# Block 1 of a two-layer kernel: a unit's first outputs move into the next step, v is transposed one key step later, and TensorE's order is tied to the step list

## The chip, the cores and the metric

The kernel runs on one core of a Trainium2 chip. A core has TensorE (matmuls, shown as PE in the profile, with its weight loads as PEld), VectorE (DVE), ScalarE (ACT), GpSimd (POOL), and SyncE (SP), whose queue issues the DMAs here. The engines run independently, each through its own instructions in a fixed order, and wait for one another by semaphores. SBUF is the working memory; TensorE writes its results to PSUM, which has eight banks. The metric is device time of one execution in microseconds, less is better.

## What is computed

Two layers over x of 4 sequences of 256 tokens, 512 wide: a gated linear attention with decay, a router with a bias mix, a state-space mixer and an adapter layer. The change is in the first, "block 1":

```python
q = (hidden_states @ Wq.T).reshape(B, L, H, D)          # H = 32 heads, D = 128
k = (hidden_states @ Wk.T).reshape(B, L, KVH, D)        # KVH = 8
v = (hidden_states @ Wv.T).reshape(B, L, KVH, D)
q, k = _apply_rope(q, cos, sin), _apply_rope(k, cos, sin)
dt = jax.nn.softplus(hidden_states @ Win.T + dt_bias)
g = dt * -jnp.exp(A_log_bias)
G = cumsum of g within chunks of 128
scores = einsum('bhnid,bhnjd->bhnij', q, k)
decay = where(causal, exp(G_i - G_j), 0)
y_intra = einsum('bhnij,bhnjd->bhnid', scores * decay, v * dt)
y = y_intra + (what earlier chunks carry over, with its decay)
y = y / sqrt(mean(y * y) + eps) * gnorm_w
gate = (hidden_states @ Wg.T).reshape(B, L, H, D)
y = y * silu(gate)
return y.reshape(B, L, H * D) @ Wo.T                    # added to x
```

With two chunks in a sequence, the carry-over of the second chunk is written as one more block of scores with its own decay.

## The kernel before

**Arithmetic.** Matrices are split into a high and a low part in a reduced fp32 format, and a product is three matmuls (high·high, high·low, low·high). `split` (line 128) makes the parts of a weight: a cast on ScalarE (line 135), a subtraction on GpSimd (line 138). `Weights` (line 142) is a list in order of use; a call such as `u.w.o()` splits everything up to that weight and starts the loads of the next two (lines 169 to 178). The step W does nothing in block 1, since `due` stays at −1 there.

**Units and steps.** Block 1 is `retention` (line 299). The tokens are in two halves of 512. A unit is a key/value group g, a pair of heads hp of its four, and a half: 32 units. For g below 5 the halves alternate; for the last three groups all units of half 0 come first, then all of half 1 (lines 460 to 468). The loop at line 495 goes over steps i from −1 to 32, with `before`, `u` and `after` the units i−1, i and i+1, and walks through a list of step names, `STEP1`, or `SIDE1` while there is side work (`k.side`):

- S0, S1, S2 (`scores`, line 387): a block of scores of u in six matmuls, into PSUM tag y; VectorE multiplies them into the decays `m` (line 400).
- A0, A1 (`value`): `attend` multiplies by v into tag g (line 408); `square` takes ScalarE's squares, GpSimd's power and VectorE's product `yr` (lines 421 to 426).
- N0, N1 (`norm`): four transposes into tag y (line 433), VectorE's product with the gate `r` (line 436), a cast on ScalarE and a subtraction (lines 439, 440).
- F (`finish(u, 0)`) and C (`finish(before, 1)`): 12 matmuls with Wo in two groups of tag o (line 452) and two VectorE additions to x (line 456). F is in u's own step, C in the next one.
- K: one step of `keys` (line 356) for `after`, where it needs a new k and v: first the k projection and its rotation, then the v projection, its copy to SBUF (line 363) and four transposes (line 366) with a copy (line 368).
- Q0, Q1 (`queries`): projection of `after`'s queries (12 matmuls at line 197, tag x), rotation by three VectorE operations and a GpSimd addition (`rope`, lines 341 to 354), and a cast and a subtraction into the one tile `qs`.
- G0, G1 (`gate`): projection of `after`'s gates, copied by ScalarE (line 383); U is their silu; D (`ready`, `decays`) loads cumulated decays to all partitions (`gb`, line 283), adds and masks them into `m` and takes the exponential (line 376).
- P and T (`k.pump`): a step of side work: the router of a finished half and the preparation of the next block, put into `k.side` by `close` when a half is done (from step 26 on).

**What sets the order.** The program is traced in the order above; a scheduler then places every instruction on its engine by a simulated timeline: among those whose inputs and buffers are free, the one that comes first in the program. So program order is a priority, and the order that an engine gets can be another one. Tiles of a pool and tag share a number of buffers; each PSUM tag (x, y, g, o) has two banks. ScalarE's functions through `k.act` (line 1111) are tied to program order in groups: silu needs one function table, exp and ln another, a table load (line 1115) stands at each change, and `behind` (line 1106) keeps each group behind the load and the load behind the group before it. `order` (line 1099) is how such a tie is made: it binds the scheduler and adds no semaphore.

Of the kernel before, what the change touches and what calls it, by code (L numbers as in the profile page):

```python
# [18 lines left out]
P = 128  # L19
# [10 lines left out]
AHEAD = 0  # L30
BANK1, BANK3 = "o", "x"
LATE = (0, 3)
STEP1 = "S0 S1 S2 W C K P A0 A1 K Q0 T P W Q1 W K P N0 G0 P W N1 G1 U T W F T D".split()
SIDE1 = "S0 T S1 P S2 W C P K A0 T A1 K Q0 P W T Q1 W P K N0 G0 P T N1 G1 U W T P F T D W".split()
STEP3 = "W T0 T1 B I0 W M0 M1 X0 X1 I1 O0 G0 W W O1 W W P O2 W W G1 P W O3 D0 D1 W W".split()
FILL3 = "B X0 X1 I0 I1 P P G0 G1 W W P P W D0 D1 E E".split()
SIDE3 = "T0 T1 I0 I1 M0 M1 P B X0 X1 P P O0 W O1 G0 G1 W W P O2 O3 W P W P D0 D1 E E".split()
# [147 lines left out]
def chunk(w, n):  # L185

    return [part[:, n, :].rearrange("p (c m) -> p c m", c=KC) for part in w]


def proj(k, tc, w, half, name, tag="x"):  # L190

    ps = k.psum.tile([P, FREE], F32, tag=tag, name=f"ps_{name}")
    x = k.xs[half]
    terms = [(w[0], x[0]), (w[0], x[1]), (w[1], x[0])]
    for c in range(KC):
        for n, (a, b) in enumerate(terms):
            tc.nc.tensor.matmul(  # L197
                ps, a[:, c, :], b[:, c, :], start=(c == 0 and n == 0), stop=(c == KC - 1 and n == 2)
            )
    return ps  # L200


# [96 lines left out]
def retention(k, tc, io, arrive, begun, done, tail):  # L299
# [3 lines left out]
    nc = tc.nc  # L303
    NH, NG = 32, 8
    with ExitStack() as st:
# [5 lines left out]
        n = 2 * NH * 2  # L311
        at = 2 * SEQ
# [43 lines left out]
        def keys(g, half, w):  # L356

            nm = f"{g}_{half}"
            kk = [k.wk.tile([P, FREE], F32R, tag="a", name=f"k{part}_{nm}", bufs=4) for part in "hl"]
            rope(proj(k, tc, chunk(w, 0), half, f"k_{nm}"), *kk, f"k_{nm}")  # L360
            yield
            vT = k.wk.tile([P, FREE], F32, tag="sq", name=f"vT_{nm}", bufs=1)
            nc.scalar.copy(vT, proj(k, tc, chunk(w, 1), half, f"v_{nm}"))
            ps = k.psum.tile([P, HT, P], F32, tag="x", name=f"ps_vt_{nm}")
            for t in range(HT):
                nc.tensor.transpose(ps[:, t, :], vT[:, t * P:t * P + P], k.ident)
            v = k.wk.tile([P, HT, P], F32, tag="sg", name=f"v_{nm}", bufs=4)
            nc.scalar.copy(v, ps)
            kv[half] = kk, v
            yield  # L370
# [7 lines left out]
        def queries(u, w, h):  # L378
            nm = f"q_{u.name}_{h}"
            rope(proj(k, tc, chunk(w, h), u.half, nm), qs[:, 0, h, :], qs[:, 1, h, :], nm)  # L380
# [6 lines left out]
        def scores(u, blk):  # L387

            kh, kl = u.kk
            zj, zi = ((0, 0), (1, 1), (0, 1))[blk]  # L390
            ps = k.psum.tile([P, 4, P], F32, tag="y", name=f"ps_sc_{u.name}_{blk}")
            for b in range(2):
                aj = slice((2 * b + zj) * P, (2 * b + zj) * P + P)
                ai = slice((2 * b + zi) * P, (2 * b + zi) * P + P)
                for i, (a, q) in enumerate(((kh, 0), (kh, 1), (kl, 0))):
                    nc.tensor.matmul(  # L396
                        ps[:, b::2, :], a[:, aj], qs[:, q, :, ai], start=(i == 0), stop=(i == 2)
                    )
            m = u.m[:, blk]
            nc.vector.tensor_tensor(m, m, ps, ALU.mult)  # L400

        def attend(u, z):
            blocks = (((0, 0),), ((0, 2), (1, 1)))[z]
            nm = f"{u.name}_{z}"
            ps = k.psum.tile([P, 4, P], F32, tag="g", name=f"ps_y1_{nm}")
            for q in range(4):
                for i, (zj, blk) in enumerate(blocks):
                    nc.tensor.matmul(  # L408
                        ps[:, q, :], u.m[:, blk, q, :], u.v[:, 2 * (q % 2) + zj, :],
                        start=(i == 0), stop=(i == len(blocks) - 1),  # L410
                    )
            u.ps_y[z] = ps

        def square(u, z):
# [13 lines left out]
        def norm(u, z):  # L428

            nm = f"{u.name}_{z}"  # L430
            ps_t = k.psum.tile([P, 4, P], F32, tag="y", name=f"ps_yt1_{nm}")
            for q in range(4):
                nc.tensor.transpose(ps_t[:, q, :], u.yr[z][:, q, :], k.ident)
            r = k.wk.tile([P, 4, P], F32, tag="yh", name=f"r1_{nm}", bufs=YB)
            sg = u.sg.rearrange("p h (b z l) -> p z (h b) l", b=2, z=2)[:, z]
            nc.vector.scalar_tensor_tensor(r, ps_t, gnorm, sg, ALU.mult, ALU.mult)
            hi = k.wk.tile([P, 4, P], F32R, tag="y", name=f"yh1_{nm}", bufs=4)
            lo = k.wk.tile([P, 4, P], F32R, tag="y", name=f"yl1_{nm}", bufs=4)
            nc.scalar.copy(hi, r)
            nc.vector.tensor_tensor(lo, r, hi.bitcast(F32), ALU.subtract)  # L440
            u.y[z] = hi, lo

        def finish(u, z):
            wh, wl = u.w.o()
            yh, yl = u.y[z]
            for b in range(2):
                t = HT * u.half + 2 * b + z
                ps = k.psum.tile([P, HID], F32, tag="o", name=f"ps_o1_{u.name}_{z}{b}")
                i = 0
                for h in range(2):  # L450
                    for y, w in ((yh, wh), (yh, wl), (yl, wh)):
                        nc.tensor.matmul(  # L452
                            ps, y[:, 2 * h + b, :], w[:, h, :], start=(i == 0), stop=(i == 5)
                        )
                        i += 1
                nc.vector.tensor_add(k.x[t], k.x[t], ps)

# [2 lines left out]
        for gs in [[g] for g in range(NG - LONE1)] + [range(NG - LONE1, NG)]:  # L460
# [3 lines left out]
            for g, hp, half in unit:  # L464
                u = Ctx()
                u.g, u.hp, u.half, u.h0, u.name = g, hp, half, 4 * g + 2 * hp, f"{g}_{hp}_{half}"
                u.ps_y, u.yr, u.y = {}, {}, {}
                units.append(u)

        before, uses = None, []  # L470
        gnorm = k.small([P, 1], "gnorm")
        for n, u in enumerate(units):

            if before is not None and (before.g, before.hp) == (u.g, u.hp):
                u.w = before.w
            else:
                u.w = w = Ctx()
                at = u.g, u.hp
                if u.hp == 0:
                    uses.append((n - 1, 0, w, "kv", io["L0_kv"][u.g], u, "w"))  # L480
                uses.append((n - 1, 1, w, "q", io["L0_attn_Wq"][at], u, "w"))
                uses.append((n - 1, 2, w, "g", io["L0_attn_Wg"][at], u, "w"))
                uses.append((n, 3, w, "o", io["L0_attn_Wo"][at], u, "wo"))
            before = u

        for _, _, w, n, src, u, tag in sorted(uses, key=lambda one: one[:2]):
# [8 lines left out]
        for i in range(-1, len(units) + 1):  # L495
            before, u, after = (
                units[j] if 0 <= j < len(units) else None for j in (i - 1, i, i + 1)
            )
# [40 lines left out]
            def gate(u, h):  # L539
                if h == 0:  # L540
                    u.sg = only.tile([P, 2, FREE], F32, tag="sg", name=f"sg1_{u.name}")
                gates(u, u.w.g(), h, "x" if i >= 0 else "g")
# [4 lines left out]
            def value(z):  # L547
# [3 lines left out]
            k.bank = BANK1  # L551
            step = dict(
                S=lambda z: scores(u, z), G=lambda h: i < 0 or gate(after, h), U=silu, A=value,
                N=lambda z: norm(u, z), F=lambda: finish(u, 0), C=close,
                Q=lambda h: queries(after, after.w.q(), h),
                K=lambda: next(new, None), D=ready, P=k.pump, T=lambda: k.pump(1, True),
                W=k.weights.step,
            )
            if i < 0:
                gate(after, 0)  # L560
                gate(after, 1)
            for one in SIDE1 if k.side else STEP1:
                if tail and u is units[-1] and one in ("Q0", "G1", "Q1", "F"):
                    tail(("Q0", "G1", "Q1", "F").index(one))
                if tail and before is units[-1] and one in ("S1", "C"):
                    tail(("S1", "C").index(one) + 4)
                if u is None and one in ("P", "T") and i > 0:
                    continue
                who = {"C": before, "Q": after, "G": after, "U": after, "K": after, "D": after, "P": k, "T": k, "W": k}.get(one[0], u)
                if who is not None:  # L570
                    step[one[0]](*(int(z) for z in one[1:]))
            if i == 0:
                begun()

# [517 lines left out]
def tile_two_layers(ctx: ExitStack, tc: tile.TileContext, io: dict, out: bass.AP):  # L1092
    nc = tc.nc
    k = Ctx()
# [4 lines left out]
    def order(ins, before, reason):  # L1099
        tc.add_manual_dep(  # L1100
            ins.ins, before.ins.name,
            mybir.DependencyInfo(mybir.DependencyClass.NoSync, mybir.DependencyReason.DATA),
            reason=reason,
        )
# [30 lines left out]
            else:  # L1135
                steps -= 1

    k.act, k.small, k.pump, k.behind = act, small, pump, order
    k.n = 0
    k.const = ctx.enter_context(tc.tile_pool(name="const", bufs=1))  # L1140
    k.smalls = ctx.enter_context(tc.tile_pool(name="smalls", bufs=3))
    k.dram = ctx.enter_context(tc.tile_pool(name="dram", bufs=1, space=bass.MemoryType.DRAM))
# [14 lines left out]
    with tc.tile_pool(name="work", bufs=2) as k.wk:  # L1157

        k.room = k.wk.tile([P, 8 * SEQ], F32, tag="big", name="room")
        of = Ctx()  # L1160
# [92 lines left out]
```

## Time and profile before

| | |
|---|---|
| median of three runs | 2557.03 us (2550.06 to 2557.84) |
| the profiled execution | 2556.84 us, span 2555.1 us |
| mean granted TensorE clock | 0.987 |
| block 1 on TensorE | about 16 to 916 us |
| table loads of ScalarE | 193, 1.28 us each |
| DMA | 206 MB, 81 GB/s, engines busy 27% of the span |

The profile is one execution. Busy time is the time in which an engine was executing; matmuls overlap one another, so their mean duration (391 to 406 ns for 512 columns) is longer than the distance from one to the next (0.227 us at full clock). An idle time is put down to the instruction that ended it. The granted clock is the share of full speed at which TensorE was allowed to run. In block 1 matmuls of 512 columns are the bulk: queries, gates and outputs have 24 of them each in a unit.

### The profile page before, as it was taken

The numbers are of one execution on the slowest core, as the hardware profiler recorded it, in microseconds if no ns is written. First come the engines' busy times: TensorE is split into PE (matmuls) and PEld (weight loads), VectorE is DVE, ScalarE is ACT, GpSimd is POOL, SyncE is SP. The second block draws the span as 40 slices with busy tenths as digits, with TensorE's granted clock in tenths as the row PEclk, the third lists the DMA queues.
The fourth block names the chain that finished last, engine by engine and source line by source line (L and its number), as shares of the span: only waits on it lengthen the run. The fifth ranks groups of instructions, "written<-read, shape, count | busy, mean of one in ns | idle before, by whom it ended". The sixth has DMA issues, their size and how long they took to land.

```text
span 2555.1 us, 36947 instructions
## 1 busy us (share of the span) xinstructions
PE 2433.6 (95%) x14000; PEld 2009.3 (79%) x14000; DVE 2016.4 (79%) x2629; ACT 1475.9 (58%) x2365; POOL 1582.3 (62%) x1123
## 2 busy tenths in 40 slices
PE   7999999999989888899999999999999999999889
PEld 6888888887777776678878888888888888888677
DVE  7766666676668678688998988988988988989973
ACT  3645555555554545475765756656757656757631
POOL 4744645466566457576775774766856865857850
PEclk9999999999999998899999999999999999999999
DMA  3311212122231222232332232323223323223321
GB/s 107 106 53 42 67 50 66 50 73 85 83 89 48 70 84 86 76 120 74 99 97 69 84 90 80 95 67 99 87 79 92 90 67 91 92 71 110 92 79 68
DMA packets 82898, 206.26 MB, mean 81 GB/s; under 512 B 8673, under 2 KB 10593, under 8 KB 82721
## 3 DMA queue, kind: packets, MB, share of 16 engines
q1 hardware_dynamic: 82720, 203.90, 26.6%
q8 instruction: 111, 1.82, 0.3%
q14 instruction: 67, 0.54, 0.1%
HBM read 200.86 MB, written 3.01 MB: 80 GB/s over the span
## 4 chain that ended last, share of the span: by engine, by line
PE 61%; DVE 18%; POOL 9%; ACT 6%; issue 5%; DMA 1%; SPq 0%; POOLq 0%; ACTq 0%; DVEq 0%
PE ps_g L197 13%; PE ps_x L197 8%; PE ps_o L854 8%; PE ps_o L452 6%; PE ps_q L197 5%; DVE m L753 4%; DVE conv L712 4%; PE ps_y L800 3%; PE ps_bc L197 3%; PE ps_sc L396 3%; PE ps_y L408 2%; PE ps_o L1080 2%; DVE yl L819 2%; DVE m L290 2%; POOL xs L814 2%
## 5 line engine op out<-in xcount | busy, mean ns | idle before, releaser
L197 PE MATMUL ps_g<-xs_hi,wg_h 128*128 128x512 f32 x768 | 305.6, 398 | 6.5 <-ACT wg_h L135 2.8
L753 DVE TENSOR_TENSOR m<-m,cb 128x1536 f32<-128x1536 f32 x128 | 274.2, 2146 | 40.0 <-ACT m L1118 39.3
L197 PE MATMUL ps_g<-xs_lo,wg_h 128*128 128x512 f32 x768 | 300.5, 391 | 0.0
L197 PE MATMUL ps_g<-xs_hi,wg_l 128*128 128x512 f32 x768 | 298.8, 391 | 0.0
L712 DVE SCALAR_TENSOR_TENSOR conv<-ps_x,cw,conv 128x510 f32<-128x510 f32 (+2 forms) x384 | 269.8, 736 | 19.6 <-ACT conv L710 17.0
L1115 ACT ACT_TABLE_LOAD x193 | 247.6, 1283 | 3.9 <-PEq L1241 0.8
L854 PE MATMUL ps_o<-wo_h,yh 128*128 128x512 f32 x512 | 211.5, 413 | 22.3 <-DVE acc L860 21.0
L290 POOL TENSOR_TENSOR m<-gb,start 128x512 f32<-128x512 f32 x128 | 150.6, 1179 | 129.3 <-PE ps_y L800 93.0
L814 POOL TENSOR_TENSOR xs<-xs,sg 128x512 f32<-128x512 f32 x128 | 207.8, 1623 | 33.5 <-DVE xs L810 32.6
L138 POOL TENSOR_TENSOR wo_l<-raw_wo,wo_h 128x1024 fp32r<-128x1024 f32 x60 | 149.9, 2499 | 106.9 <-ACT wo_h L135 95.8
L828 POOL TENSOR_TENSOR sqs<-sqs,sq 128x512 f32<-128x512 f32 x112 | 193.6, 1729 | 34.8 <-ACT sq L826 34.8
L854 PE MATMUL ps_o<-wo_h,yl 128*128 128x512 f32 x512 | 198.5, 402 | 5.0 <-DVE yl L819 5.0
L197 PE MATMUL ps_x<-xs_lo,wx_h 128*128 128x512 f32 x512 | 202.5, 396 | 0.0
L197 PE MATMUL ps_x<-xs_hi,wx_h 128*128 128x512 f32 x512 | 201.9, 394 | 0.4 <-DVE conv L712 0.2
L854 PE MATMUL ps_o<-wo_l,yh 128*128 128x512 f32 x512 | 202.1, 395 | 0.0
L197 PE MATMUL ps_x<-xs_hi,wx_l 128*128 128x512 f32 x512 | 201.3, 393 | 0.0
L1118 ACT ACTIVATE xs<-conv,cb 128x512 f32<-128x512 f32 x128 | 90.8, 723 | 190.7 <-DVE conv L712 190.5
L292 POOL TENSOR_SCALAR_AFFINE_SELECT m<-m 128x1024 f32<-128x1024 f32 x160 | 198.6, 1242 | 1.4 <-DVE m L290 1.3
L138 POOL TENSOR_TENSOR wg_l<-raw_wg,wg_h 128x1024 fp32r<-128x1024 f32 x60 | 149.8, 2496 | 70.5 <-ACT wg_h L135 66.4
L138 POOL TENSOR_TENSOR wx_l<-raw_wx,wx_h 128x1024 fp32r<-128x1024 f32 x38 | 95.5, 2513 | 154.4 <-ACT wx_h L135 141.6
L800 PE MATMUL ps_y<-m,xd 128*64 128x128 f32 x2048 | 177.6, 279 | 13.7 <-DVE m L753 7.2
L1118 ACT ACTIVATE m<-m 128x1024 f32<-128x1024 f32 (+1 forms) x160 | 181.7, 1135 | 6.7 <-POOL m L292 6.4
(276 smaller groups left out, 6860.4 us busy)
## 6 DMA issues: line engine op xcount, KB each, us to landing
gb<-cum SPq DMA_DIRECT2D x160, 512.0 KB
raw_wx<-in_L_attn_in_x_dram SPq DMA_DIRECT2D x38, 512.0 KB
raw_wg<-in_L_attn_in_gate_dram SPq DMA_DIRECT2D x38, 512.0 KB
raw_wo<-n_L_attn_out_proj_w_dram SPq DMA_DIRECT2D x38, 512.0 KB
raw_wq<-in_L_attn_Wq_dram SPq DMA_DIRECT2D x22, 512.0 KB
raw_wg<-in_L_attn_Wg_dram SPq DMA_DIRECT2D x22, 512.0 KB
raw_wo<-in_L_attn_Wo_dram SPq DMA_DIRECT2D x22, 512.0 KB
raw_wkv<-in_L_kv_dram SPq DMA_DIRECT2D x11, 512.0 KB
```

What stands on the lines that cost most here:

```text
L138: nc.gpsimd.tensor_tensor(lo, w, hi.bitcast(F32), ALU.subtract)
L197: tc.nc.tensor.matmul(ps, a[:, c, :], b[:, c, :], start=(c == 0 and n == 0), stop=(c == KC - 1 and n == 2))
L290: engine.tensor_tensor(m[:, blk], gb[:, min(blk, 1)], last(at, P), ALU.add)
L292: nc.gpsimd.affine_select(out=causal, in_=causal, compare_op=ALU.is_ge, fill=GONE, base=0, pattern=[[0, 8], [1, P]], channel_multiplier=-1,)
L712: nc.vector.scalar_tensor_tensor(acc[:, :, j:], ps[:, :, :SEQ - j], cw[:, ch, TAPS - 1 - j:TAPS - j], acc[:, :, j:], ALU.mult, ALU.add,)
L753: made = nc.vector.tensor_tensor(mh, mh, cbs[p.g, p.half].rearrange("p z b l -> p z (b l)").unsqueeze(2) .to_broadcast([P, 3, 2, 2 * P]), ...
L800: one = nc.tensor.matmul(ps_y[h * D:h * D + D, 2 * b + z, :], p.xe[:, n, b, h, :] if blk == 2 else xd[:, 2 * b + zs, h, :], m[:, blk, 2 * ...
L814: nc.gpsimd.tensor_tensor(xs, xs, p.sg[n], ALU.mult)
L828: nc.gpsimd.tensor_tensor(total, total, sq, ALU.add)
L854: nc.tensor.matmul(ps, y[:, at], w[:, n, :], start=(i == 0), stop=(i == 5))
L1115: load = nc.scalar.preload_act_table_set(table)
L1118: ins = nc.scalar.activation(out, in_, func, bias=bias, scale=scale)
```

## The change

The two lists get a new order: F leaves the end of the step and stands behind the scores of the next one, ahead of C and for `before` instead of `u`; G0 comes before N0 and the third K before G0. P, T and W steps are placed anew. `keys` stops once more, between the copy of v and its transposes, so that these belong to the third K. In the list of weights, Wo's place of use changes from (n, 3) to (n + 1, −1). And TensorE is tied: every matmul and transpose of `proj`, `keys`, `scores`, `attend`, `norm` and `finish` goes through `k.line`, which puts the first one of a step S, F, C, A, Q, K, G or N behind the last one of such a step before it.

```diff
-STEP1 = "S0 S1 S2 W C K P A0 A1 K Q0 T P W Q1 W K P N0 G0 P W N1 G1 U T W F T D".split()
-SIDE1 = "S0 T S1 P S2 W C P K A0 T A1 K Q0 P W T Q1 W P K N0 G0 P T N1 G1 U W T P F T D W".split()
+STEP1 = "S0 S1 S2 W F C K P A0 A1 K Q0 P W Q1 K W T G0 N0 P W N1 G1 U T W P D".split()
+SIDE1 = "S0 S1 S2 P F C W K P A0 A1 K P Q0 W P Q1 K T W G0 N0 T P W N1 G1 U T T T D W".split()
...
@@ proj (and in the same way line 366, scores, attend, norm, finish)
-            tc.nc.tensor.matmul(
+            k.line(tc.nc.tensor.matmul(
                 ps, a[:, c, :], b[:, c, :], start=(c == 0 and n == 0), stop=(c == KC - 1 and n == 2)
-            )
+            ))
...
@@ keys
             nc.scalar.copy(vT, proj(k, tc, chunk(w, 1), half, f"v_{nm}"))
+            yield
             ps = k.psum.tile([P, HT, P], F32, tag="x", name=f"ps_vt_{nm}")
...
-                uses.append((n, 3, w, "o", io["L0_attn_Wo"][at], u, "wo"))
+                uses.append((n + 1, -1, w, "o", io["L0_attn_Wo"][of], u, "wo"))
...
-                N=lambda z: norm(u, z), F=lambda: finish(u, 0), C=close,
+                N=lambda z: norm(u, z), F=lambda: finish(before, 0), C=close,
...
+                    k.follow = at.last if i >= 0 and one[0] in "SFCAQKGN" else None
                     step[one[0]](*(int(z) for z in one[1:]))
+                    if i >= 0 and one[0] in "SFCAQKGN":
+                        if k.follow is None:
+                            at.last = k.done
+                        k.follow = None
...
+    def line(ins):
+        if k.follow is not None:
+            order(ins, k.follow, "order of the steps")
+            k.follow = None
+        k.done = ins
```

`at` is a new holder whose `last` starts as None. P, T, U, D and W are not tied, nor is anything at step −1.

More of the change, by code (lines that the diff above doesn't have):

```diff
@@ L363, in keys @@
             nc.scalar.copy(vT, proj(k, tc, chunk(w, 1), half, f"v_{nm}"))
+            yield
             ps = k.psum.tile([P, HT, P], F32, tag="x", name=f"ps_vt_{nm}")
             for t in range(HT):
-                nc.tensor.transpose(ps[:, t, :], vT[:, t * P:t * P + P], k.ident)
+                k.line(nc.tensor.transpose(ps[:, t, :], vT[:, t * P:t * P + P], k.ident))
             v = k.wk.tile([P, HT, P], F32, tag="sg", name=f"v_{nm}", bufs=4)
@@ L395, in scores @@
                 for i, (a, q) in enumerate(((kh, 0), (kh, 1), (kl, 0))):
-                    nc.tensor.matmul(
+                    k.line(nc.tensor.matmul(
                         ps[:, b::2, :], a[:, aj], qs[:, q, :, ai], start=(i == 0), stop=(i == 2)
-                    )
+                    ))
             m = u.m[:, blk]
@@ L407, in attend @@
                 for i, (zj, blk) in enumerate(blocks):
-                    nc.tensor.matmul(
+                    k.line(nc.tensor.matmul(
                         ps[:, q, :], u.m[:, blk, q, :], u.v[:, 2 * (q % 2) + zj, :],
                         start=(i == 0), stop=(i == len(blocks) - 1),
-                    )
+                    ))
             u.ps_y[z] = ps
@@ L432, in norm @@
             for q in range(4):
-                nc.tensor.transpose(ps_t[:, q, :], u.yr[z][:, q, :], k.ident)
+                k.line(nc.tensor.transpose(ps_t[:, q, :], u.yr[z][:, q, :], k.ident))
             r = k.wk.tile([P, 4, P], F32, tag="yh", name=f"r1_{nm}", bufs=YB)
@@ L451, in finish @@
                     for y, w in ((yh, wh), (yh, wl), (yl, wh)):
-                        nc.tensor.matmul(
+                        k.line(nc.tensor.matmul(
                             ps, y[:, 2 * h + b, :], w[:, h, :], start=(i == 0), stop=(i == 5)
-                        )
+                        ))
                         i += 1
@@ L468, in retention @@
                 units.append(u)
+        at = Ctx()
+        at.last = None
         before, uses = None, []
@@ L477, in retention @@
                 u.w = w = Ctx()
-                at = u.g, u.hp
+                of = u.g, u.hp
                 if u.hp == 0:
                     uses.append((n - 1, 0, w, "kv", io["L0_kv"][u.g], u, "w"))
-                uses.append((n - 1, 1, w, "q", io["L0_attn_Wq"][at], u, "w"))
-                uses.append((n - 1, 2, w, "g", io["L0_attn_Wg"][at], u, "w"))
-                uses.append((n, 3, w, "o", io["L0_attn_Wo"][at], u, "wo"))
+                uses.append((n - 1, 1, w, "q", io["L0_attn_Wq"][of], u, "w"))
+                uses.append((n - 1, 2, w, "g", io["L0_attn_Wg"][of], u, "w"))
+                uses.append((n + 1, -1, w, "o", io["L0_attn_Wo"][of], u, "wo"))
             before = u
@@ L568, in retention @@
                     continue
-                who = {"C": before, "Q": after, "G": after, "U": after, "K": after, "D": after, "P": k, "T": k, "W": k}.get(one[0], u)
+                who = {"C": before, "F": before, "Q": after, "G": after, "U": after, "K": after, "D": after, "P": k, "T": k, "W": k}.get(one[0], u)
                 if who is not None:
+                    k.follow = at.last if i >= 0 and one[0] in "SFCAQKGN" else None
                     step[one[0]](*(int(z) for z in one[1:]))
+                    if i >= 0 and one[0] in "SFCAQKGN":
+                        if k.follow is None:
+                            at.last = k.done
+                        k.follow = None
             if i == 0:
@@ L1136, in pump @@
                 steps -= 1
-    k.act, k.small, k.pump, k.behind = act, small, pump, order
-    k.n = 0
+    def line(ins):
[3 more added lines that the diff above has]
+        k.done = ins
+    k.act, k.small, k.pump, k.behind, k.line = act, small, pump, order, line
+    k.n, k.follow, k.done = 0, None, None
     k.const = ctx.enter_context(tc.tile_pool(name="const", bufs=1))
```

## The prediction

> **What bounds the kernel now.** The page's busy line first, then the stretch of block 1 away from its ends:
>
> ```profile
> PE 2433.6 (95%) x14000; PEld 2009.3 (79%) x14000; DVE 2016.4 (79%) x2629; ACT 1475.9 (58%) x2365; POOL 1582.3 (62%) x1123
> ...
> 75.00:690.00 615.00, 591.73 (x3158) 502.00 (x3157) 412.93 (x558) 335.00 (x687) 349.16 (x277) 1.00 0.23 67
> ```
>
> TensorE is the bound: 95% of the span, and 591.7 of 615 us here (columns: length, busy TensorE, weight loads, VectorE, ScalarE, GpSimd, granted clock, DMA share, GB/s). So the change can only win what TensorE idles in block 1, and loses whatever idling it adds. The waits of TensorE between 50 and 920 us (total, times, longest):
>
> ```profile
> PE ps_vt L366 <- ACT vT L363: 14.1, 12, 1.9
> PE ps_yt L433 <- DVE yr L426: 8.2, 6, 3.5
> PE ps_sc L396 <- DVE r L436: 3.7, 8, 0.5
> ...
> PE ps_o L452 <- ACT yh L439: 3.0, 2, 1.5
> ```
>
> All waits of that answer sum to 47 us; that is nearly the whole prize. The v transpose, right behind the projection it needs, has the largest share.
>
> Next, in what order TensorE works today. The chain of waits from 266 us (start, length):
>
> ```profile
> 266.00 2.72 PE ps_q L197 x12
> 268.72 1.59 PE ps_g L197 x7
> 270.31 0.44 PE ps_yt L433 x4
> 270.75 0.71 PE ps_sc L396 x6
> 271.46 3.87 PE ps_g L197 x17
> 275.32 1.43 PE ps_sc L396 x12
> 276.76 2.75 PE ps_o L452 x12
> 279.50 0.89 PE ps_y L408 x8
> ```
>
> This is not the step list's order (S, C, A, Q, G). The queries' casts on ScalarE come at 277.09, right after the scores end, because `qs` has one buffer; so the Q and G at 266 to 275 us belong to the unit after the one whose scores stand at 270 to 276. The scheduler has moved Q and G of the next unit ahead of this unit's scores. ScalarE's timeline shows what that hides:
>
> ```profile
> 276.62 0.57 ACT L383 COPY sg<-ps_g 128x512 f32<-128x512 f32 x1
> 277.09 1.14 ACT L353 CAST qs<-r_q 128x512 fp32r<-128x512 f32 x2
> 278.13 1.06 ACT L1118 ACTIVATE sg<-sg 128x1024 f32<-128x1024 f32 x1
> 279.20 1.28 ACT L1115 ACT_TABLE_LOAD   x1
> 280.49 1.49 ACT L1118 ACTIVATE m<-m 128x1536 f32<-128x1536 f32 x1
> ```
>
> A unit's decays `m` are exponentiated only behind the silu of the same unit's gates (line 1118 in program order: U before D, with a table load between), so only after its G1. The scores that use this exponential start at 294.47 us, 12.5 us after it ends: ample slack, because other units' work stands between.
>
> **The change, part by part.** 32 units; a step is about 25.6 us (46 table loads, two a unit, from 100 to 690 us: 23 units in 590).
>
> *v later* (yield before line 364): moves four transposes and one ScalarE copy per k/v behind Q1; nothing added. It removes the 14.1 us. But the x tag has two PSUM banks, and the order becomes v, Q0, Q1, vt, G0: G0 needs Q1's bank (three VectorE reads of 0.69 from Q1's end, 2.15 us) or vt's (copy of 0.59 behind transposes of 0.66). TensorE has only vt to do meanwhile: idle 0.7 us by the nearer bank, 1.6 by the other, over the 14 steps of the loop with keys. I take 0.7, since a tile may take whichever of its tag's banks is free first: **+10 us, bounds 0 (VectorE done early enough) and 22**.
>
> *Outputs moved.* F's 12 matmuls and two VectorE adds (0.65 each) are the same work elsewhere. r, the cast and the subtraction (0.75 + 0.62 + 0.68) now lie under G1 and the scores. Its call also brings the weight split: cast 1.05 on ScalarE, 2.40 on GpSimd, and up to two loads on SP (0.33 us issue each) that now stand behind `gb`'s. SP issued six DMAs in 45 us, so that is free; the order of weights is unchanged (n, 3 and n+1, -1 are neighbours). The split needs only a raw tile loaded two weights ahead and a free slot, and ScalarE is idle 42%: nothing. If it falls behind the exponential, F, due at 5.28 + 0.9 = 6.2 us after G1 by the count below, waits 4.5 + 1.05 + 2.4 − 6.2 = 1.8 us in 15 steps: bounds **0 and 27 us**.
>
> *The tie.* Each S, F, C, A, Q, K, G, N step starts behind the last matmul of the step before in list order; there are no new instructions or semaphores. TensorE then runs G1 of unit u+1, S0, S1, S2 with nothing between. The scores use tag y, two banks: S0 and S1 fill them, and S2 waits for VectorE's product of S0 with `m`, line 400, which waits for the exponential above. Counted from the end of G1: copy starts at 0.04 and takes 0.59, silu by 1.07, load by 1.29, exponential 1.49: 4.50; product 0.05 + 0.68; next matmul 0.05: **5.28 us**. S0 and S1 take 1.43 (the row of 12 above). Idle: **3.85 us per step**. Behind S2 on TensorE are F, C, A0, A1, Q and G; all are tied, so none can fill it. Steps 1 to 26 have no side work: 26 × 3.85 = 100. In steps 27 to 31 (the router and the next block's preparation, not tied) I take 1.5 each, between 0 and 3.85: 8. **+108 us**; bounds 100, and 152 if a weight cast of 1.05 gets between (31 × 4.9).
>
> The other chains fit: Q1's end to S0 is three products, GpSimd 1.28, cast 0.62, subtraction 0.69, about 4.7 to 5.3 us, against G0, N0, N1, G1 = 6.3; a lateness of up to 3.8 us more hides in the same stall. From A1 to N1, squares 3.2, GpSimd 1.3, product 0.69 = 5.2 lie under Q0, Q1, G0 = 8.2.
>
> *The clock.* Idling of this length has been paid twice in this trace. Behind the wait of 1.86 us that ended at 708.59:
>
> ```profile
> 706.00:709.40 3.40, 1.54 (x10) 1.03 (x9) 0.86 (x1) 2.25 (x5) 3.40 (x4) 1.00 0.37 135
> 709.40:712.80 3.40, 3.40 (x10) 2.63 (x9) 0.69 (x1) 0.47 (x1) 3.40 (x4) 0.50 0.72 143
> ```
>
> The granted clock is 0.50 for 3.4 us, and matmuls start every 0.427 instead of 0.227 us: 3.4 × (1 − 0.227/0.427) = 1.6 us lost. Waits of 1.4 to 1.5 us (259.87, 364.54) cost nothing of the kind. A stall of 3.85 gives at least one such stretch, partly under the stall itself (0.7 lost) or, as after 903 us, 5.5 us of it (2.6 lost). I take 1.6 × 26 + 3 for the side steps = **+45 us; bounds 18 and 68**.
>
> *Removed:* 14.1 (vt), 3.7 (scores behind r: G1 is now between), 1.5 (one yh), 1.9 (G behind a rope, replaced above) and some 4 of yr: **−25 us, bounds −14 and −35** (of 47).
>
> [...]
> [...]
>
> **Sum**, against the profiled execution (2556.84 us; span 2555.1 and 1.7 around it, 0.2 under the median 2557.03): −25 + 10 + 108 + 45 = +138, **2695 us**. All bounds at their ends: −35 + 0 + 100 + 0 + 18 = +83 (2640) and −14 + 22 + 152 + 27 + 68 = +255 (2812).
>
> **Rivals.**
> 1. *The exponential is not late: the fixed order removes waits and adds none.* Place: S2 behind S0's product. It decides below 15/31 = 0.5 us of stall a step. For: TensorE waits 23 us in 615 today, and the list looks covered everywhere else. Against: in every unit of ScalarE's timeline read (the silu rows at 46, 74, 98, 114, 278 and 297 us), silu, load and exponential follow in that order, so nothing can bring it before G1. 2556.84 − 25 + 10 = **2542**.
> 2. *The tie does not bind* (a step's first matmul only; the scheduler still fills with what is untied). Only the v part shows: −14.1, or nothing if the bank wait eats it: **2543 to 2557**. Against: a step's later matmuls stand behind it in PSUM accumulation or by priority, and nearly all block 1 matmuls are in tied steps.
> 3. *The clock holds:* the stall without the 45 us, **2650**. For: 1.5 us waits did not drop it. Against: 1.86 did.
> 4. *More waits beside it:* weight split behind the exponential, the other bank, two clock stretches: −25 + 22 + 120 + 27 + 68 = +212, **2769**.
>
> **Numbers.** Forecast 0.52; rival 1 0.13; rival 2 0.07; rival 3 0.13; rival 4 0.15. The likeliest's own range is 2640 to 2785. Rivals 1 and 2 hold the two tenths that may be left out, so the range ends short of them at 2600 and, with rival 4, at 2800. A measurement tells about 0.3% (7.7 us). Faster: rival 1 and 0.04 of rival 2, 0.17; same 0.03; slower 0.80.
>
> **What would show it.** After: TensorE's order G1, S0, S1, wait, S2, F, C, A; a line of some 100 us, 26 or more times, of scores behind VectorE's `m` (or behind ScalarE's exponential); clock stretches of 0.5 in every slice of block 1; no wait of vt; G behind a rope or v's copy 14 times; block 1 longer by the sum and later blocks as before. Scores following each other without a wait, or an exponential ahead of G1, would make this wrong.

## The result and the profile after

The changed kernel takes **2729.10 us** (median of 4 runs, 2728.01 to 2731.40) against 2556.47 beside it: ratio **1.0682**, 95% interval 1.0662 to 1.0701, that is +172.6 us. The forecast was 2695 us. The page's busy line and the stretch from 75 to 690 us:

```profile
PE 2496.7 (92%) x14000; PEld 2055.5 (75%) x14000; DVE 2036.5 (75%) x2629; ACT 1478.3 (54%) x2365; POOL 1590.3 (58%) x1123
...
75.00:690.00 615.00, 518.66 (x2568) 437.11 (x2568) 348.10 (x458) 267.20 (x557) 273.91 (x221) 0.92 0.17 48
```

The same 615 us now hold 2568 matmuls instead of 3158, and the granted clock is 0.92 instead of 1.00. Over the whole span the 14000 matmuls are busy for 63.1 us longer (2496.7 against 2433.6), and TensorE idles 108.0 us longer (229.5 against 121.5): two costs, which add up to the span's +171.1. All of it lies in block 1: TensorE's last output there (line 453, line 452 before) ends at 1110.2 us instead of 933.7 (the table's 916 us leaves out its last outputs), and what follows takes 1616.0 us against 1621.5. TensorE's waits from 50 to 1100 us (total, times, longest) say where the idling is:

```profile
PE ps_sc L397 <- DVE m L401: 107.6, 30, 5.1
PE ps_sc L397 <- DVE qs L354: 18.6, 21, 1.4
PE ps_g L197 <- ACT v L369: 11.9, 14, 1.0
PE ps_sc L397 <- ACT qs L353: 5.9, 8, 0.8
```

Thirty of 32 units wait once in their scores for VectorE's product with the decays. G0 waits 14 times for v's bank. The v transpose's wait for its copy is gone. The chain of waits through one such step:

```profile
299.83 2.29 PE ps_g L197 x10
302.14 0.59 ACT sg L384
302.76 1.06 ACT sg L1127
303.82 1.28 ACT L1124
305.11 1.49 ACT m L1127
306.61 0.02 issue
306.63 0.70 DVE m L401
307.33 0.04 issue
307.37 1.65 PE ps_sc L397 x6
```

G1 ends at 302.10; copy, silu, table load, exponential and product follow without a gap, and S2 starts at 307.37, 5.27 us later. S0 and S1 were through at 303.53. S2's six matmuls then take 1.65 us, where S1's six took 0.9 (302.65 to 303.53); the granted clock tells why (columns: length, five engines, clock, DMA share, GB/s):

```profile
304.00:307.40 3.40, 0.03 (x1) 0.03 (x1) 0.77 (x2) 3.37 (x3) 0.00 (x0) 0.97 0.01 2
307.40:310.80 3.40, 3.40 (x11) 2.97 (x12) 1.20 (x2) 0.50 (x1) 0.00 (x0) 0.53 0.00 0
```

In other steps ScalarE stands in the way first. Its timeline in the step after:

```profile
337.37 1.04 ACT L135 CAST wkv_h<-raw_wkv 128x1024 fp32r<-128x1024 f32 x1 [0.22 <-DMA raw_wkv<-in_L_kv_dram]
338.32 0.58 ACT L384 COPY sg<-ps_g 128x512 f32<-128x512 f32 x1
338.94 1.06 ACT L1127 ACTIVATE sg<-sg 128x1024 f32<-128x1024 f32 x1
340.00 1.28 ACT L1124 ACT_TABLE_LOAD   x1
341.30 1.48 ACT L1127 ACTIVATE m<-m 128x1536 f32<-128x1536 f32 x1
```

A weight's cast goes ahead of G1's copy, so S2 starts only at 343.56, 6.7 us after G1's end at 336.87; S0 has waited 1.43 us for the queries and S2 waits 3.58, together 5.0.

### The profile page after: what moved, and what is told of

It is laid out like the page before. It is cut to its first block, busy times and chain, and to the rows that moved or that the text cites. A ratio compares the mean times of both kernels' runs of the same rounds, so it can differ in the third digit from the quotient of the medians.

```text
span 2726.2 us, 36921 instructions
## 1 busy us (share of the span) xinstructions
PE 2496.7 (92%) x14000; PEld 2055.5 (75%) x14000; DVE 2036.5 (75%) x2629; ACT 1478.3 (54%) x2365; POOL 1590.3 (58%) x1123
## 4 chain that ended last, share of the span: by engine, by line
PE 48%; DVE 23%; POOL 11%; ACT 10%; issue 5%; DMA 2%; POOLq 0%; SPq 0%; ACTq 0%; DVEq 0%
PE ps_g L197 8%; PE ps_o L453 7%; PE ps_x L197 7%; PE ps_o L863 7%; DVE m L762 4%; DVE conv L721 4%; PE ps_y L809 3%; ACT m L1127 3%; PE ps_bc L197 2%; ACT L1124 2%; DVE m L290 2%; POOL ms L425 2%; DVE yl L828 2%; PE ps_sc L397 2%; PE ps_o L1089 2%
## 5 line engine op out<-in xcount | busy, mean ns | idle before, releaser
L197 PE MATMUL ps_g<-xs_hi,wg_h 128*128 128x512 f32 x768 | 308.5, 402 | 14.2 <-ACT v L369 11.9
L422 ACT ACTIVATE sq<-ps_y 128x128 f32<-128x128 f32 x256 | 71.1, 278 | 305.4 <-PE ps_y L409 299.8
L863 PE MATMUL ps_o<-wo_h,yh 128*128 128x512 f32 x512 | 212.3, 415 | 17.2 <-DVE acc L869 15.9
L397 PE MATMUL ps_sc<-qs,kh 128*128 128x256 f32 x384 | 99.8, 348 | 134.7 <-DVE m L401 107.6
L397 PEld LDWEIGHTS ps_sc<-qs,kh 128*128 128x128 f32 x384 | 74.8, 232 | 154.8 <-DVE m L401 110.2
```

The costliest lines, as they stand in the source:

```text
L197: k.line(tc.nc.tensor.matmul(ps, a[:, c, :], b[:, c, :], start=(c == 0 and n == 0), stop=(c == KC - 1 and n == 2)))
L397: k.line(nc.tensor.matmul(ps[:, b::2, :], a[:, aj], qs[:, q, :, ai], start=(i == 0), stop=(i == 2)))
L863: nc.tensor.matmul(ps, y[:, at], w[:, n, :], start=(i == 0), stop=(i == 5))
```

## The experiments

| kernel | median, us | ratio to before | 95% interval |
|---|---|---|---|
| changed | 2729.10 | 1.0682 | 1.0662 to 1.0701 |
| e1: changed, untied | 2531.94 | 0.9898 | 0.9883 to 0.9913 |
| e2: before, tie alone | 2664.59 | 1.0417 | 1.0397 to 1.0437 |
| e3: changed, D ahead of G0 | 2618.81 | 1.0235 | 1.0220 to 1.0250 |
| e4: changed, S2 behind C | 2569.30 | 1.0043 | 1.0027 to 1.0058 |
| e5: changed, stall filled | 2686.82 | 1.0504 | 1.0489 to 1.0518 |
| e6: before, v later alone | 2555.76 | 0.9999 | 0.9991 to 1.0008 |
| e7: before, D ahead alone | 2533.27 | 0.9909 | 0.9893 to 0.9925 |
| e8: before, F moved alone | 2541.59 | 0.9940 | 0.9926 to 0.9954 |
| e9: changed, untied, D ahead | **2505.68** | 0.9798 | 0.9785 to 0.9811 |
| e10: changed, D ahead and S2 behind C | 2573.76 | 1.0064 | 1.0045 to 1.0084 |

**Untied (e1).** The changed kernel without the one call that binds:

```diff
         if k.follow is not None:
-            order(ins, k.follow, "order of the steps")
             k.follow = None
```

> The changed kernel with only the tie taken out: lists, F's place and the later v stay. Theory (the tie is the cause, by putting S2 right behind G1 while its decays still wait for the exponential): the scheduler moves Q and G ahead of the scores again, the wait of scores behind VectorE's m falls from 107.6 us to under 10, and the time is 2535 to 2565 us. Rival (F's move and the new lists cost by themselves): 2650 us or more.

2531.94 us, 3 below the range given: on these lists the tie alone makes 197 us of difference, and everything else in the change gains some 26 (ratio 0.9898). No wait of scores behind `m` is left; the two longest kinds of wait in block 1 (50 to 1000 us):

```profile
PE ps_yt L434 <- DVE yr L427: 6.3, 10, 1.5
...
PE ps_sc L397 <- DVE r L437: 3.7, 5, 2.3
```

And TensorE's order is again that of before, projections first (from its chain of waits):

```profile
301.97 4.13 PE ps_q L197 x18
306.10 0.91 PE ps_o L453 x4
307.01 2.72 PE ps_g L197 x12
309.73 1.82 PE ps_o L453 x8
311.55 0.44 PE ps_yt L434 x4
311.98 0.71 PE ps_sc L397 x6
312.69 2.73 PE ps_g L197 x12
315.43 1.43 PE ps_sc L397 x12
```

The queries' casts come at 316.95 us, right after these scores end, so the Q and G in front belong to the next unit.

**Tie alone (e2).** The kernel before with `k.line` around the same matmuls, its own lists, F at the end of its own step, v as it was.

> The kernel before with only the tie added: old lists, F at the end of its own step, v transposed at once. Theory: F's 2.72 us now stand between G1 and S0, so S2 waits 5.28 - 2.72 - 1.43 = 1.1 us, and 1 to 2 with weight casts in front of the exponential, in 31 steps: +35 to +60 us, no clock loss, v's wait stays (14 us): 2580 to 2620 us. Rival (the tie costs the same wherever F stands): 2700 us or more.

2664.59 us, between the two: 45 above the theory's range and 35 below the rival's. Where F stands matters, but it covers less than the theory had. The waits from 50 to 1000 us:

```profile
PE ps_sc L396 <- DVE m L400: 43.3, 26, 4.1
PE ps_vt L366 <- ACT vT L363: 16.2, 14, 1.4
PE ps_sc L396 <- DVE qs L354: 14.1, 10, 1.6
PE ps_sc L396 <- ACT qs L353: 13.0, 10, 4.0
```

The quiet steps have the 1.13 us that were worked out; every fourth step waits 3.1 to 3.3 us behind weights' casts (up to 4.1 late in the block), and S0's waits for the queries (27 us) were not in the forecast. TensorE's busy time is 41 us above that of before, and the mean granted clock 0.971 against 0.987: the clock fell here too, which the theory had ruled out. With F between G1 and S0 the scores' waits behind `m` are 64 us shorter than in the changed kernel (107.6 − 43.3); the two kernels differ in the place of G0, in v's transposes and in P and T as well, so not all of that need be F's.

**The exponential ahead (e3).** D, with the exponential, ahead of G0, so that it is tied behind the silu of the unit before:

```diff
-... Q1 K W T G0 N0 P W N1 G1 U T W P D
+... Q1 K D W T G0 N0 P W N1 G1 U T W P
-... Q1 K T W G0 N0 T P W N1 G1 U T T T D W
+... Q1 K D T W G0 N0 T P W N1 G1 U T T T W
```

> The changed kernel, tie and all, with D ahead of G0 in both lists, so that the exponential of the decays no longer stands behind the silu of the same unit's gates. Theory (the stall is silu, table load and exponential behind G1): scores behind m falls from 107.6 us to under 10, the half-clock stretches go, and the time is 2530 to 2570 us. Rival (a fixed order stalls anyway, other waits take the place): 2640 us or more.

2618.81 us, between the two ranges: 110 us less than the changed kernel, and the scores' wait behind `m` falls from 107.6 to 27.8 us, not under 10 (7.4 of it in one early step). The stretches at half clock up to 1100 us fall from 177 to 82 us and do not go (mean granted clock 0.977, against 0.959 in the changed kernel). Theory and rival hold in part. The chain of waits in one of the steps that still stall:

```profile
299.59 1.55 POOL wg_l L138
301.14 0.76 issue
301.90 1.76 POOL r_q L351
303.69 0.63 ACT qs L353
304.34 2.21 DVE qs L354
306.55 3.38 DVE yl L441 x2
309.93 0.61 DVE m L401
310.58 0.98 PE ps_sc L397 x6
```

No exponential is in it. GpSimd splits a weight in front of the queries' rotation. VectorE's subtractions of the queries' and outputs' low parts then fall beside two more such splits (303.61 to 306.01 and 306.61 to 309.39 us): one of each takes 2.21 and 2.86 us, against a median of 0.69 for both. Only then does VectorE multiply the scores. S0 waits 1.41 us and S2 2.41, in one step of four. In the changed kernel S2's part of this lateness lay under the exponential's stall; it shows when that is taken away.

**S2 behind F and C (e4).**

```diff
-STEP1 = "S0 S1 S2 W F C K ...
+STEP1 = "S0 S1 W F C S2 K ...
-SIDE1 = "S0 S1 S2 P F C W K ...
+SIDE1 = "S0 S1 P F C S2 W K ...
```

> The changed kernel with S2 behind F and C in both lists; the exponential stays late. Theory (only S2 is held, because S0 and S1 fill both banks of tag y): F and C, 5.4 us, cover a wait of 3.8 to 5.7 us, the rest is 0 to 0.5 us a step, no clock loss: 2540 to 2580 us. Rival (the wait is for something that F and C need too, or A takes it over): 2640 us or more.

2569.30 us, as the theory gave. The exponential still stands behind G1 and the silu, but only S2 has to wait until the product of S0 frees a bank: with 24 matmuls in front of it, no wait of scores behind `m` is left. The stretches at half clock up to 1100 us sum to 55 us, near the 51 of before (mean granted clock 0.986 against 0.987). What is left of waits in the changed kernel's rows:

```profile
PE ps_sc L397 <- DVE qs L354: 15.6, 19, 1.4
PE ps_g L197 <- ACT v L369: 11.9, 14, 1.0
```

**The stall filled (e5).** S1's six matmuls are issued six times, with the same values into the same bank, so that TensorE works through the stall; the result is the same:

```diff
+                for again in range(6 if blk == 1 else 1):
                     for i, (a, q) in enumerate(((kh, 0), (kh, 1), (kl, 0))):
```

> The changed kernel with the six matmuls of S1 issued six times over (same values into the same bank; no part of the result changes), so that TensorE works through 3.6 us of each stall. S2 still starts 5.2 us after G1. Theory (the stall is paid twice, the second time by the clock: TensorE's busy time rose by 63 us for the same 14000 matmuls): the half-clock stretches behind the scores go and the time falls by 45 to 65 us, to 2660 to 2685 us. Rival (the clock costs nothing beside the wait): 2715 to 2745 us.

2686.82 us, 42 less than the changed kernel, 2 outside the range given. Its waits (the line numbers are one higher):

```profile
PE ps_sc L398 <- ACT qs L353: 14.3, 10, 8.0
PE ps_sc L398 <- DVE m L402: 9.7, 18, 1.0
```

S2 starts as late as in the changed kernel (5.28 us behind G1 in a quiet step), yet the time falls: that part is the clock. Behind S2's start at 304.88 it holds:

```profile
304.90:308.30 3.40, 3.40 (x18) 2.95 (x19) 1.89 (x3) 0.50 (x1) 0.00 (x0) 1.00 0.00 0
```

In the trace's record the stretches at 0.50 up to 1100 us sum to 177 us in the changed kernel, 51 in the kernel before and 20 here (mean granted clock 0.959, 0.987 and 0.989). Why 42 us and not 63 can be worked out: the 960 added matmuls start every 0.120 us, an estimated 115 us of busy time. Without them TensorE's 2550.6 us are 2435, against 2433.6 before, so some 61 of the 63 us of clock come back. But TensorE's idle time falls by 99 us only, 16 less than the fill adds: the fill does not fit every stall, and scores wait 8.4 us more for ScalarE's queries (14.3 against 5.9), one wait of 8.0 alone.

**The parts alone (e6, e8).** The kernel before with the `yield` behind v's copy only:

> The kernel before with only the stop between v's copy and its transposes. Theory: v's wait of 14 us goes, G0 waits for a bank of tag x in part of the steps, and free scheduling fills some of that: 5 to 14 us faster than before. Rival (the bank's wait eats it all): within 3 us of before.

No difference (2555.76 us against 2556.65 beside it): the rival holds. The wait of v is gone from the rows, and others have its place (50 to 1000 us):

```profile
PE ps_yt L433 <- DVE yr L426: 8.2, 6, 3.5
```

stood before; now there are

```profile
PE ps_yt L434 <- DVE yr L427: 11.8, 10, 3.8
PE ps_o L453 <- ACT yh L440: 10.6, 9, 1.7
PE ps_g L197 <- ACT v L369: 5.5, 6, 2.0
PE ps_g L197 <- DVE r_q L350: 4.9, 4, 1.8
```

With F moved only (`finish(before, 0)` behind S2 in both lists, and Wo's place of use):

> The kernel before with only F moved behind the scores of the next step (and Wo's place in the list). Theory: free scheduling moves it where there is room; the waits of scores behind r (3.7 us) and outputs behind yh (1.5) go: 3 to 15 us faster than before. Rival (F is missed as filler between G1 and the scores): slower than before.

2541.59 us, 15 less than before, at the theory's upper end: in the free order F's new place gains. The v transposes' wait for their copy falls with it from 14.1 to 4.8 us, which the theory had not named; the rest was not followed up.

**The best version (e9), and what D does alone (e7).** e9 is e1 and e3 together; e7 moves D ahead of N0 and G0 in the kernel before.

> The changed kernel without the tie and with D ahead of G0, so that no scores wait for the exponential and nothing fixes TensorE's order. Theory: without the tie the exponential was already 12 us early, so D's place matters little: 2515 to 2545 us, as the untied kernel (2532) or a little better. Rival (D's early place takes ScalarE or GpSimd time from the rotation): 2550 us or more.

> The kernel before with only D moved ahead of N0 and G0 in both lists (no tie, F and v as before). Theory (free scheduling with F moved is what gains, D ahead adds what it added there, 26 us): 2520 to 2545 us. Rival (the exponential was 12 us early in the kernel before, so D's place is worth nothing without F's move): within 5 us of before.

e9 takes 2505.68 us, 2.0% less than before and 9 below the range given; e7 gains 23. So D's place is worth 23 to 26 us with or without F's move, although no scores waited for the exponential: the theory "it was early anyway" falls, and e7's rival with it. TensorE has almost no idle time left (e9, 300 to 400 us):

```profile
300.00:400.00 100.00, 99.31 (x536) 85.18 (x535) 70.31 (x96) 55.67 (x117) 53.91 (x44) 1.00 0.21 58
```

Which instruction the scheduler places better by it was not tried and stays open.

**Both cures under the tie (e10).**

> The changed kernel, tied, with D ahead of G0 and S2 behind F and C. Theory (with S2 behind C the exponential was already covered; what the tie still costs are the waits of S0 for the rotated queries, some 16 us, and of G0 for v's copy, 12 us, which D's place does not touch): 2555 to 2580 us, as with S2 behind C alone (2569). Rival (the two cures add up): 2530 us or less.

2573.76 us: they do not add up, and the tied kernel stays 68 us above the best free one (e9, whose S2 stands ahead of F and C). Its waits are S0's for the queries (17.2 us), G0's for v's copy (12.0), a single 9.4 us for a weight's cast in the first steps, and

```profile
PE ps_o L453 <- DVE x L457: 9.0, 11, 1.0
```

outputs for their own bank. In e9's rows the same three kinds are 3.6, 1.8 and 0 us.

## Why the prediction was right

- **The bound and the order before.** That the scheduler had moved Q and G ahead of the scores, and that the tie undoes it, is shown by e1: its order, and 197 us between bound and free.
- **S2's stall.** 5.28 us from G1's end to S2 were worked out from rows of before, and 5.27 were seen in a quiet step; 3.85 idle, 3.84 seen (177, 307, 437 us). That only S2 is held, by two banks, is shown by e4; that the exponential's place is the cause, by e3's 110 us.
- **The size of it** was too small: 108 us forecast, 132 measured (107.6 + 18.6 + 5.9). The term that failed is the 3.85 us for each of the 26 steps without side work. Nine of them wait 3.81 to 3.84 us. In sixteen, every second one up to 603 us and every one from 655 us on, one or two weights' casts go ahead of G1's copy, and the scores wait 4.8 to 6.2 us; the prediction had a cast in the upper bound only. The 26 steps sum to 123 us instead of 100. The five steps with side work (scores from 929 us on) wait 0.4, 3.0, 0.9, 3.2 and 0 us, 7.5 in all, as the 8 that were taken.
- **The other chains** ("a lateness of up to 3.8 us more hides in the same stall") did hide in the quiet steps, but e3 shows that they do not fit the list by themselves: the working, 4.7 to 5.3 us against 6.3, left out the weight splits on GpSimd, in front of the rotation (2.41 us at 299.55) and beside VectorE's subtractions (2.21 and 2.86 us there, against a median of 0.69).
- **Outputs moved:** nothing taken; one wait of 0.2 us for F's weight split is in the rows.
- **G0's bank:** +10 forecast, 11.9 in 14 waits, by the nearer bank as taken.
- **The clock:** +45 forecast; TensorE's busy time rose by 63, and e5 shows that nearly all of it hangs on the stalls. The size was low because only the nine stalls of 3.8 us are followed by 3.4 us at 0.50, as taken; the sixteen longer ones are followed by 6.8, the two stretches of rival 4. The reading that waits of 1.4 to 1.5 us cost no clock has an exception in the trace of before: behind waits of 1.51 us (ended at 687.54) and 0.33 us, 3.4 us at 0.50 begin at 688.9. So the length of one wait does not settle it.
- **What is removed:** −25 forecast. All waits of before summed to 47 us; the changed kernel's, without the four rows shown, sum to 20, so 27 went. The v transposes' 14.1 are among them, but G0's 11.9 took their place, as the two terms say together; v's later place alone is worth nothing in the free order too (e6).
- **Idle and clock in sum:** −25 + 10 + 108 = +93 idle against 108 measured, +45 busy against 63. Both misses have the same sign, so the forecast did not come out by errors that cancel.

## What to carry to other kernels

Before fixing an engine's order by hand, look in the trace at what the free order hides: here it had pulled the next unit's projections in front of a chain of five instructions on ScalarE and VectorE, and no row of waits showed that chain. Tie only what must be tied, and where a late result holds the banks, put work that needs no such bank ahead of the step that waits (e4: 2569.30 us against 2729.10). When a wait is taken away, look for the lateness that lay under it (e3: 27.8 us of the 107.6 stayed). And look for a stall's price in two places, in the wait and in the granted clock after it: here 108 us more of idling and 63 us more of busy time for the same 14000 matmuls.

## What the runs showed of the hardware

In the changed kernel's record of the granted clock each of the nine stalls of 3.81 to 3.84 us is followed by 3.4 us at half clock (from 307.2 us on, for one), and each of the sixteen of 4.8 to 6.2 us by 6.8 us, which begin while S2 still waits (from 341.3 us on, S2 at 343.56). With TensorE kept at work through the same wait (e5), on matmuls that nobody needs, the stretches at half clock up to 1100 us fall from 177 to 20 us and the kernel is 42 us faster. In e3, VectorE's subtractions of 128x512 took 2.21 and 2.86 us where GpSimd was splitting a weight, against a median of 0.69 between 300 and 400 us. Each ended 0.54 us after the split beside it: at 306.55 behind 306.01, and at 309.93 behind 309.39.
